# Column attention and feed-forward stage: three column groups in work in a turn instead of two

## The chip, the cores and the metric

The kernel runs on one core of a Trainium2 chip. The metric is the device time of one execution in microseconds (us), the median of several runs. Each engine of the core has its own instruction queue and works through it in order: TensorE (PE; its weight loads are listed as PEld), VectorE (DVE), ScalarE (ACT), GpSimd (POOL) and SyncE (SP). POOL and SP issue the DMA transfers here.

## The reference, cut to what matters

The whole program has two layers on an input of 4 x 64 x 256 x 256 (fp32): a convolutional layer with attention and a gated feed-forward part, and a layer with row attention, column attention and a feed-forward part. The change is in the last stage, which computes this part of the second layer (`h` has batch 4, 256 rows, 256 columns and 64 channels):

```python
def _lin_attn(x, wq, bq, wk, bk, wv, bv, wo, bo):     # 4 heads, one q and one k value a head
    q = elu(x @ wq.T + bq) + 1
    k = elu(x @ wk.T + bk) + 1
    v = x @ wv.T + bv
    q = q / q.mean(axis=3, keepdims=True)             # over the positions of a column
    k = k / k.sum(axis=3, keepdims=True)
    ktv = einsum('brhcd,brhce->brhde', k, v)
    o = einsum('brhcd,brhde->brhce', q, ktv)
    return o @ wo.T + bo

hc = _ln(h.swapaxes(1, 2), cn_g, cn_b)                # columns
h = h + _lin_attn(hc, col_wq, ...).swapaxes(1, 2)
f = _ln(h, fn_g, fn_b)
f = gelu(f @ w1.T + b1) @ w2.T + b2                   # 64 -> 256 -> 64 channels
return moveaxis(h + f, -1, 1)                         # channels first
```

## The kernel before, in words

The program is one function with stages after each other: `stage_a` with the attention and local parts of the first layer, `stage_c1` and `stage_c2` for its feed-forward part, `stage_c3` for the row attention, and `stage_d` for column attention, feed-forward and output. Only `stage_d` differs. `stage_c3` leaves `h` in DRAM as `hd`; `stage_d` reads it.

The stage works on groups of 32 columns: 8 groups in each of 4 batches, 32 groups in all (`seq`: batch `b`, group `g`). A tile `h` holds one group: 128 partitions (rows of one half), 32 columns, two row halves (`rh`) and 64 channels. For each group:

- `load` (L1168): four transfers of 512 KB from SP's queue bring the tile `h`.
- `attn` (L1193): in eight steps the tile is transposed by TensorE (L1203), copied by ScalarE (L1205, `xT`) and multiplied with the query and key weights (L1212, `qk`); beside it `spread` on VectorE takes the mean off 16 x 64 elements at a time and sums the squares (L1178 sum, L1180 centring, L1182 square on ScalarE, L1183 sum of squares). `rstd` (L1186) takes root and reciprocal. Then come the features (`f`, `kz`, L1229 and L1232; the exponential is L696), the product of keys and values (L1238), the sums (L1242), a transpose of q (L1245), the column's small matrix (`zn`, L1259, `mix` with L702, `bdm` L1265), and for each row half the result (a bias product L1271, the product L1274) that is added into `h` in place (L1277). At the end `spread` and `rstd` again give the normalized tiles `xf` (L1288).
- `ffn` (L1291): in eight steps `first` transposes a quarter of `xf` (L1298) and copies it (L1300, `xfT`); four products with `w1` (L1311) go through gelu on ScalarE (L1313, `hg`); `y` takes the transposed `h` (L1319) and the products of `hg` with `w2` (L1322), and VectorE adds the bias and writes it into the output tile `st` (L1324), four columns at a time, with a stride.

`attn` and `ffn` are generators. In turn `n` the main loop (L1342) runs the attention of group `n` and the feed-forward of group `n - 1` in alternation, from one `yield` to the next (`_steps`). A tile framework sets the final order of the instructions on each engine, adds the waits, and gives tiles their buffers: `mm` has six PSUM buffers, `sm` two, `h` three, `xf` five, most others two. In a step of `ffn` the second product takes the gelu values of the same step; the transposes of the next step stand between the two. `st` holds two groups (64 columns); after the second, eight transfers from POOL's queue (L1347) write it out, each of 64 partitions x 32 rows x 64 floats (runs of 256 B).

Of the kernel before, what the change touches and what calls it, by code (L numbers as in the profile page):

```python
# [9 lines left out]
F32 = mybir.dt.float32  # L10
AF = mybir.ActivationFunctionType
ALU = mybir.AluOpType
# [237 lines left out]
def kernel(ctx: ExitStack, tc: tile.TileContext, x, packs, fd, out, off):  # L250
# [8 lines left out]
    def mm():  # L259
        return ps.tile([128, 512], F32, tag="mm", name="mm")  # L260

    def sm():
        return ps.tile([128, 512], F32, tag="sm", name="sm", bufs=2)
# [33 lines left out]
    def bc(ap, n):  # L297

        return ap.unsqueeze(2).to_broadcast([ap.shape[0], ap.shape[1], n])
# [839 lines left out]
    def stage_d():  # L1139
        with ExitStack() as cs:  # L1140
# [25 lines left out]
            V.memset(one, 1.0)  # L1166

            def load(b, g):  # L1168
                h = p.tile([128, 32, 2, C], F32, name="h", bufs=3)
                for rh in (0, 1):  # L1170
                    for j in (0, 1):
                        SY.dma_start(h[:, 16 * j:16 * j + 16, rh, :], hd[b, rh * 128:(rh + 1) * 128, :, 2 * g + j, :])
                return h

            def spread(src, n, s2):

                s1 = p.tile([128, n], F32, tag="ln_s", name="ln_s")
                V.tensor_reduce(s1, src, AX.X, ALU.add)  # L1178
                xc = p.tile([128, n, C], F32, tag="xc", name="xc")
                V.scalar_tensor_tensor(xc, bc(s1, C), -LN_S, src, ALU.mult, ALU.add)  # L1180
                sq = p.tile([128, n, C], F32, tag="ln_sq", name="ln_sq")
                S.activation(sq, xc, AF.Square)  # L1182
                V.tensor_reduce(s2, sq, AX.X, ALU.add)  # L1183
                return xc

            def rstd(s2, n):  # L1186
                s3 = p.tile([128, n], F32, tag="ln_d", name="ln_d")
                S.activation(s3, s2, AF.Sqrt, bias=eps_t, scale=LN_S)
                s4 = p.tile([128, n], F32, tag="ln_r", name="ln_r")
                V.reciprocal(s4, s3)  # L1190
                return s4

            def attn(h, xfs):  # L1193

                qp = p1.tile([128, 32, 32], F32, name="qp")
                v1 = p1.tile([128, 64], F32, name="v1")
                for r in range(8):
                    if r % 2 == 0:
                        k = r // 2
                        spread(h[:, 8 * k:8 * k + 8].rearrange("p c a e -> p (c a) e"), 16, v1[:, 16 * k:16 * k + 16])  # L1200
                    t = mm()
                    for i in range(4):
                        T.transpose(t[:, i * 128:(i + 1) * 128], h[:, r * 4 + i].rearrange("p a e -> p (a e)"), ident)  # L1203
                    xT = p.tile([128, 512], F32, name="xT")
                    S.copy(xT, t)  # L1205
                    yield
                    if r % 4 == 0:
                        qk = sm()


                    for g in range(4):
                        T.matmul(qk[g * 32:(g + 1) * 32, r % 4 * 128:r % 4 * 128 + 128], cwt, xT.rearrange("p (c n) -> p c n", c=4)[:, :, g * 32:(g + 1) * 32],  # L1212
                                 start=True, stop=True)
                    if r % 4 == 3:

                        V.transpose(qp[:, r // 4 * 16:r // 4 * 16 + 16].rearrange("p c m -> p (c m)"), qk)
                rs = rstd(v1, 64)
                u = qp[:, :, 0:16].rearrange("p c (r k) -> p c r k", r=2)
                V.tensor_tensor(u, u, bc4(rs, 2, 8), ALU.mult)
                V.tensor_tensor(u, u, cbq.unsqueeze(1).unsqueeze(1).to_broadcast([128, 32, 2, 8]), ALU.add)  # L1220
                yield
                e = feature(p1, u, [128, 32, 2, 8])
                yield
                f = p1.tile([128, 2, 2, 32, 4], F32, name="f")
# [2 lines left out]
                for rh in (0, 1):  # L1227
                    for k in (0, 1):
                        V.scalar_tensor_tensor(f[:, rh, k], uv[:, rh, :, k * 4:k * 4 + 4], 1.0, ev[:, rh, :, k * 4:k * 4 + 4], ALU.add, ALU.max)  # L1229
                fv = f.rearrange("p r k c h -> p r k (c h)")  # L1230
                kz = p1.tile([128, 2, 128], F32, name="kz")
                V.tensor_tensor(kz.rearrange("p r (c h) -> p r c h", h=4), f[:, :, 1], rs.rearrange("p (c r) -> p r c", r=2).unsqueeze(3).to_broadcast([128, 2, 32, 4]), ALU.mult)  # L1232
                yield

                t = mm()
                for rh in (0, 1):
                    for g in range(4):
                        T.matmul(t[g * 32:(g + 1) * 32, :], kz[:, rh, g * 32:(g + 1) * 32], h[:, 8 * g:8 * g + 8, rh, :], start=(rh == 0), stop=(rh == 1))  # L1238
                qs = sm()
                for k in (0, 1):  # L1240
                    for rh in (0, 1):
# [36 lines left out]
                    yield  # L1278
                for hf in (0, 1):
                    v2 = p.tile([128, 32], F32, name="v2")  # L1280
                    xcs = []
                    for k in (2 * hf, 2 * hf + 1):
                        xcs.append(spread(h[:, 8 * k:8 * k + 8].rearrange("p c a e -> p (c a) e"), 16, v2[:, (k % 2) * 16:(k % 2) * 16 + 16]))
                        yield
                    rs = rstd(v2, 32)
                    for k in (0, 1):
                        xf = p.tile([128, 8, 2, C], F32, name="xf", bufs=5)
                        V.tensor_tensor(xf.rearrange("p c a e -> p (c a) e"), xcs[k], bc(rs[:, k * 16:k * 16 + 16], C), ALU.mult)  # L1288
                        xfs.append(xf)

            def ffn(h, xfs, st, gi):  # L1291


                def first(r):
                    t = mm()
                    xf = xfs[r // 2]
                    for i in range(4):
                        T.transpose(t[:, i * 128:(i + 1) * 128], xf[:, (r % 2) * 4 + i].rearrange("p a e -> p (a e)"), ident)  # L1298
                    xT = p.tile([128, 512], F32, name="xfT")
                    S.copy(xT, t)  # L1300
                    return xT

                yield
                xT = first(0)
                for r in range(8):
                    yield
                    hg = []
                    for i in (0, 1):
                        for rh in (0, 1):
                            t = mm()  # L1310
                            T.matmul(t, w1[rh * 64:(rh + 1) * 64, i * 128:(i + 1) * 128], xT[rh * 64:(rh + 1) * 64], start=True, stop=True)  # L1311
                            g = p.tile([128, 512], F32, tag=f"hg{rh}{i}", name=f"hg{rh}{i}")
                            S.activation(g, t, AF.Gelu, bias=b1[:, i:i + 1])  # L1313
                            hg.append(g)
                    nx = first(r + 1) if r < 7 else None
                    yield
                    y = mm()
                    for i in range(4):
                        T.matmul(y[:, i * 128:(i + 1) * 128], h[:, r * 4 + i].rearrange("p a e -> p (a e)"), ident, is_transpose=True, start=(i == 0), stop=False, skip_group_check=True)  # L1319
                    for i in (0, 1):  # L1320
                        for rh in (0, 1):
                            T.matmul(y[rh * 64:(rh + 1) * 64, :], w2[:, i, :], hg[i * 2 + rh], start=False, stop=(i == 1), skip_group_check=True)  # L1322
                    c = gi * 32 + r * 4
                    V.tensor_scalar(st[:, :, c:c + 4].rearrange("p r c -> p c r"), y.rearrange("p (c r) -> p c r", c=4), K("b2"), None, ALU.add)  # L1324
                    xT = nx

            seq = [(b, g) for b in range(B) for g in range(8)]
            hs = {0: load(*seq[0])}
            xfs = {}
            st = None  # L1330
            for n in range(len(seq) + 1):
                if n + 1 < len(seq):
                    hs[n + 1] = load(*seq[n + 1])
                xfs[n] = []
                ga = attn(hs[n], xfs[n]) if n < len(seq) else None
                gf = None
                if n >= 1:
                    b, g = seq[n - 1]
                    if g % 2 == 0:
                        st = p.tile([128, 128, 64], F32, name="st")  # L1340
                    gf = ffn(hs.pop(n - 1), xfs.pop(n - 1), st, g % 2)
                _steps(ga, gf)  # L1342
                if n >= 1 and g % 2 == 1:
                    for i in range(4):
                        for rh in (0, 1):
                            r = rh * 128 + i * 32
                            G.dma_start(out[b, :, r:r + 32, g // 2 * 64:g // 2 * 64 + 64], st[rh * 64:(rh + 1) * 64, i * 32:(i + 1) * 32])  # L1347

    stage_d()

# [19 lines left out]
```

## Time and profile before

| | |
|---|---|
| time, median of 3 runs | 8939.46 us (8939.42 to 8940.79) |
| profiled execution, its own time | 8937.15 us |
| its span in the profile | 8935.4 us |
| granted TensorE clock, mean | 0.971 |
| begin of the last stage's first load | 6680.0 us |
| last copy into `st` begins | 8907.2 us |
| first of the last eight output issues | 8908.7 us |
| output transfer, issue to landing, median | 13.2 us |

A time in the profile is counted from the start of the span. The page gives busy time by engine for the whole program; a query of stretches gives it for chosen windows; the timeline gives the instructions of an engine in order, with the idle time before each and the engine and line whose end ended it. One group of the last stage takes 68.3 us; the examples are taken from the turn that begins at about 7699 us and the one after it.

### The profile page before, as it was taken

How to read it: one execution, taken by the hardware profiler on the slowest of the kernel's cores; microseconds unless marked ns; L12 is line 12 of the kernel's file. 1: busy time of each engine (PE TensorE's matmuls, PEld its weight loads, DVE VectorE, ACT ScalarE, POOL GpSimd, SP SyncE). 2: the span in 40 equal slices, each digit the busy share in tenths (PEclk: the TensorE clock that was granted, in tenths of full speed). 3: DMA queues.
4: the chain of work that ended last, by engine and by line, in shares of the span. 5: the costliest groups of instructions: out<-in, count | busy, mean ns of one | idle time of the engine just before them, and what ended most of it. 6: DMA issues, size and time to landing. Idle time of an engine off the chain costs nothing. (4 is left out here: it accounts for less than half of the span.)

```text
span 8935.4 us, 143218 instructions
## 1 busy us (share of the span) xinstructions
PE 8237.0 (92%) x57518; PEld 4221.3 (47%) x57518; DVE 5940.4 (66%) x8506; ACT 4587.6 (51%) x7782; POOL 1133.1 (13%) x1828
## 2 busy tenths in 40 slices
PE   8999999699999998999999999999988888989897
PEld 6777777344444443333333344444443333333333
DVE  7766666377777773222222488888877888788776
ACT  4455554455555552222222366666656677667765
POOL 1111111112222221000000011111110000000000
PEclk9999999799999999999999999999998999999998
DMA  7777777799999998888888755555542233233232
GB/s 164 160 187 184 183 185 176 219 357 390 392 390 389 394 378 304 299 296 297 298 298 295 240 170 170 170 170 170 169 121 45 54 70 67 48 76 65 50 67 48
DMA packets 1258502, 1832.48 MB, mean 205 GB/s; under 512 B 335600, under 2 KB 1040112, under 8 KB 1196656
## 3 DMA queue, kind: packets, MB, share of 16 engines
q1 hardware_dynamic: 1053296, 1034.63, 38.5%
q0 software_dynamic: 204544, 788.69, 27.0%
q8 instruction: 456, 7.47, 0.3%
q14 instruction: 206, 1.69, 0.1%
HBM read 967.65 MB, written 788.53 MB: 197 GB/s over the span
## 5 line engine op out<-in xcount | busy, mean ns | idle before, releaser
L915 DVE TENSOR_TENSOR y<-ge,mm 128x512 f32<-128x512 f32 (+1 forms) x640 | 406.0, 634 | 1211.8 <-ACT ge L914 1211.8
L882 PE MATMUL mm<-t,w 128*128 128x512 f32 (+1 forms) x2560 | 1093.7, 566 | 19.1 <-DMA t<-td 19.1
L914 ACT ACTIVATE ge<-mm 128x512 f32<-128x512 f32 (+1 forms) x640 | 354.7, 554 | 1253.8 <-PE mm L889 1253.8
L1313 ACT ACTIVATE hg<-mm,b 128x512 f32<-128x512 f32 x1024 | 631.7, 685 | 331.0 <-PE mm L1311 328.7
L775 PE MATMUL mm<-gp,wc 128*64 128x510 f32 (+1 forms) x3072 | 702.4, 596 | 89.0 <-DVE xm L785 51.0
L620 PEld LDWEIGHTS mm<-wqk,gp 128*128 128x128 f32 x6144 | 728.0, 197 | 99.0 <-issue 60.7
L620 PE MATMUL mm<-wqk,gp 128*128 128x128 f32 x6144 | 761.5, 282 | 1.1 <-POOL gp L589 0.9
L882 PEld LDWEIGHTS mm<-t,w 128*128 128x128 f32 x2560 | 455.2, 189 | 647.5 <-issue 436.9
L1322 PE MATMUL mm<-hg,pack_d 128*64 128x512 f32 x2048 | 579.8, 609 | 101.0 <-ACT hg L1313 101.0
L1311 PE MATMUL mm<-xfT,w 64*128 64x512 f32 x2048 | 637.7, 665 | 2.9 <-ACT xfT L1300 2.2
L830 ACT COPY tb<-mm 128x512 f32<-128x512 f32 x512 | 300.1, 587 | 631.3 <-PE mm L824 631.2
L889 PE MATMUL mm<-t,w 64*64 64x504 f32 (+1 forms) x5120 | 575.6, 555 | 0.0
L824 PE MATMUL mm<-xl,pack_c 64*128 64x512 f32 x2048 | 511.7, 601 | 6.0 <-ACT xl L812 4.6
L775 PEld LDWEIGHTS mm<-gp,wc 128*64 128x64 f32 x3072 | 277.9, 137 | 468.8 <-issue 330.8
L316 ACT ACTIVATE ln_sq<-xn 128x1024 f32<-128x1024 f32 x256 | 274.2, 1071 | 365.9 <-DVE xn L314 365.8
L318 DVE TENSOR_REDUCE ln_v<-ln_sq 128x16 f32<-128x1024 f32 x256 | 312.0, 1219 | 184.2 <-ACT ln_sq L316 184.1
L1324 DVE TENSOR_SCALAR st<-mm,pack_d 128x512 f32<-128x512 f32 x256 | 279.2, 1090 | 171.8 <-PE mm L1322 171.8
L970 PE MATMUL mm<-ya,pack_e 128*64 128x512 f32 x1024 | 381.7, 616 | 11.4 <-DMA ya<-yd 11.4
L1182 ACT ACTIVATE ln_sq<-xc 128x1024 f32<-128x1024 f32 x256 | 266.9, 1055 | 219.8 <-DVE xc L1180 219.7
L828 DVE COPY tb<-mm 128x512 f32<-128x512 f32 x512 | 344.8, 685 | 23.7 <-PE mm L824 18.2
L1311 PEld LDWEIGHTS mm<-xfT,w 64*128 64x128 f32 x2048 | 220.5, 202 | 271.5 <-issue 159.4
L889 PEld LDWEIGHTS mm<-t,w 64*64 64x64 f32 x5120 | 158.1, 132 | 374.4 <-issue 374.4
(458 smaller groups left out, 15178.4 us busy)
## 6 DMA issues: line engine op xcount, KB each, us to landing
t<-td SPq DMA_DIRECT2D x256, 1152.0 KB, 10.0
td<-tb POOLq DMA_DIRECT2D x144, 1024.0 KB, 16.1
td<-tb POOLq DMA_DIRECT2D x288, 512.0 KB, 13.9
yd<-y POOLq DMA_DIRECT2D x128, 1152.0 KB, 10.1
ya<-yd SPq DMA_DIRECT2D x192, 512.0 KB, 5.7
xs<-in_x_dram SPq DMA_DIRECT2D x128, 512.0 KB, 6.8
projd<-pj POOLq DMA_DIRECT2D x256, 256.0 KB, 6.1
gp<-projd SPq DMA_DIRECT2D x128, 512.0 KB, 9.3
```

Of the source, the lines that this page charges most:

```text
L620: T.matmul(qp[:, k * 128:(k + 1) * 128], gp[:, 2 * i + k // 2, at + dx:at + dx + 128], wqk[:, dx, :], start=(dx == 0), stop=(dx == 2))
L775: T.matmul(tv[i * 64:(i + 1) * 64, :, o], wc[2 * pr + i][:, dx, :], gps[i][:, 2 * r:2 * r + 2, i_], start=(dx == 1), stop=False, skip_grou ...
L824: T.matmul(t, inT[q, hf * 128:(hf + 1) * 128], xls[b // 2, s][q, :, 2 * y:2 * y + 2].rearrange("p f y t -> p f (y t)"), start=True, stop=True)
L828: V.tensor_copy(o, i_)
L882: T.matmul(t[:, :n], w[:, 0:128], x_[:, c, :], start=True, stop=False, skip_group_check=True)
L889: T.matmul(t[po:po + 64, :n].rearrange("p (n c) -> p n c", c=64)[:, :, o], w[q:q + 64, 128:192], x_[q:q + 64, c, i_], start=False, stop=Tr ...
L914: S.activation(ge[:, :n], ts[0][k][:, :n], AF.Gelu)
L915: V.tensor_tensor(y[:, c, :].rearrange("p n c -> p (n c)"), ge[:, :n], ts[1][k][:, :n], ALU.mult)
L970: T.matmul(t[b * 64:(b + 1) * 64, :], owT, ya[:, :, 2 * r:2 * r + 2, b * 64:(b + 1) * 64].rearrange("p f y t -> p y f t"), start=True, sto ...
L1311: T.matmul(t, w1[rh * 64:(rh + 1) * 64, i * 128:(i + 1) * 128], xT[rh * 64:(rh + 1) * 64], start=True, stop=True)
L1313: S.activation(g, t, AF.Gelu, bias=b1[:, i:i + 1])
L1322: T.matmul(y[rh * 64:(rh + 1) * 64, :], w2[:, i, :], hg[i * 2 + rh], start=False, stop=(i == 1), skip_group_check=True)
```

## The change

- `attn` is split in `scores` (transposes, `spread`, products, features up to `kz`) and `result` (from the product of keys and values to `xf`). In turn `n` the loop now runs `scores` of group `n + 1`, `result` of group `n` and the feed-forward of group `n - 1`.
- `ffn` is split in `turn` (transposes of `xf` and their copy), `first` (products with `w1`, gelu) and `second` (products with `w2`, copy into `st`). Step `i` counts through all groups; in the place of step `i` stand `turn(i + 2)`, `first(i + 1)` and `second(i)`. In `scores` the transposes of step `r + 1` stand ahead of the break in which the product of step `r + 1` follows.
- `spread` takes two chunks in one call; both sums of squares come after both centrings.
- `st` holds one group (32 columns); four transfers write it, each of 64 partitions x 64 rows x 32 floats (runs of 128 B).
- `h` has four buffers instead of three and is loaded two turns ahead; `xf` has six instead of five.

```diff
-                h = p.tile([128, 32, 2, C], F32, name="h", bufs=3)
+                h = p.tile([128, 32, 2, C], F32, name="h", bufs=4)
...
-            def spread(src, n, s2):
...
+            def spread(h, ks, v):
+                xcs, sqs = [], []
+                for k in ks:
+                    src = h[:, 8 * k:8 * k + 8].rearrange("p c a e -> p (c a) e")
+                    s1 = p.tile([128, 16], F32, tag="ln_s", name="ln_s")
+                    V.tensor_reduce(s1, src, AX.X, ALU.add)
+                    xc = p.tile([128, 16, C], F32, tag="xc", name="xc")
+                    V.scalar_tensor_tensor(xc, bc(s1, C), -LN_S, src, ALU.mult, ALU.add)
+                    sq = p.tile([128, 16, C], F32, tag="ln_sq", name="ln_sq")
+                    S.activation(sq, xc, AF.Square)
+                    xcs.append(xc)
+                    sqs.append(sq)
+                for i, k in enumerate(ks):
+                    V.tensor_reduce(v[:, 16 * i:16 * i + 16], sqs[i], AX.X, ALU.add)
+                return xcs
...
+            def scores(n):
...
+                xT = up(0)
+                spread(h, (0, 1), v1[:, 0:32])
+                yield
+                yield
+                qk = sm()
+                for r in range(7):
+                    if r == 4:
+                        back(0, qk)
+                        qk = sm()
+                    score(r, xT, qk)
+                    xT = up(r + 1)
+                    yield
+                    if r < 5:
+                        if r == 4:
+                            spread(h, (2, 3), v1[:, 32:64])
+                        yield
+                score(7, xT, qk)
+                back(1, qk)
                 rs = rstd(v1, 64)
...
+                fks[n] = f, kz
+
+            def result(n):
+                h = hs[n]
+                f, kz = fks.pop(n)
                 yield
...
+                    xcs = spread(h, (2 * hf, 2 * hf + 1), v2)
+                    yield
                     rs = rstd(v2, 32)
...
-                        xf = p.tile([128, 8, 2, C], F32, name="xf", bufs=5)
+                        xf = p.tile([128, 8, 2, C], F32, name="xf", bufs=6)
...
+            def second(i):
+                n, r = divmod(i, 8)
+                h, hg = hs[n], hgs.pop(i)
+                if r == 0:
+                    sts[n] = p.tile([128, 128, 32], F32, name="st")
...
+                V.tensor_scalar(st[:, :, 4 * r:4 * r + 4].rearrange("p r c -> p c r"), y.rearrange("p (c r) -> p c r", c=4), K("b2"), None, ALU.add)
+                if r == 7:
+                    b, g = seq[n]
+                    for q in (0, 1):
+                        for rh in (0, 1):
+                            y0 = rh * 128 + q * 64
+                            G.dma_start(out[b, :, y0:y0 + 64, g * 32:g * 32 + 32], sts[n][rh * 64:(rh + 1) * 64, q * 64:(q + 1) * 64])
...
+            for n in range(-1, N + 1):
+                if 0 <= n + 2 < N:
+                    hs[n + 2] = load(*seq[n + 2])
+                gs = scores(n + 1) if n + 1 < N else iter(())
+                gr = result(n) if 0 <= n < N else iter(())
+                for r in range(8):
+                    i = 8 * (n - 1) + r
+                    if 0 <= i + 2 < 8 * N:
+                        turn(i + 2)
+                    if 0 <= i + 1 < 8 * N:
+                        first(i + 1)
+                    next(gs, 0)
+                    next(gr, 0)
+                    if 0 <= i < 8 * N:
+                        second(i)
+                    next(gs, 0)
+                    next(gr, 0)
+                _steps(gs, gr)
```

In the changed file the lines named above have new numbers: L1203 becomes L1210, L1205 L1212, L1212 L1219, L1178 L1181, L1180 L1183, L1183 L1189, L1238 L1269, L1242 L1274, L1245 L1277, L1259 L1291, L1271 L1303, L1274 L1306, L1277 L1309, L1298 L1328, L1311 L1339, L1313 L1341, L1319 L1353, L1322 L1356, L1324 L1357, L1347 L1363.

## The prediction

> **What bounds the kernel now.** I read the page's table of engines first, then the stretches of one group each, then the timeline of VectorE and of TensorE inside one such stretch.
>
> ```profile
> span 8935.4 us, 143218 instructions
> PE 8237.0 (92%) x57518; PEld 4221.3 (47%) x57518; DVE 5940.4 (66%) x8506; ACT 4587.6 (51%) x7782; POOL 1133.1 (13%) x1828
> ```
>
> These shares are means over stages. The change is in the last stage only, which starts at 6680 us, so the stretches of that stage decide:
>
> ```profile
> core 0: us, PE busy (x) PEld busy (x) DVE busy (x) ACT busy (x) POOL busy (x), PEclk, DMA share, GB/s
> 7699.40:7767.70 68.30, 61.00 (x349) 26.78 (x349) 54.56 (x68) 47.41 (x69) 6.39 (x7) 0.97 0.44 91
> 7767.70:7836.00 68.30, 61.02 (x351) 26.84 (x351) 54.56 (x68) 47.40 (x69) 2.58 (x4) 0.97 0.15 34
> ```
>
> One column group takes 68.3 us. TensorE looks like the bound with 61.0 us, but part of that is slow clock and waits inside runs of matmuls. At its undisturbed pace (pieces of the chain of waits: L1311 1.92, L1298 0.59, L1212 0.35, L1203 0.59, L1319 0.44, L1322 1.87 us, so 5.76 for each of 8 steps; and 7.8 us for the attention product) it needs 53.9 us. VectorE needs 54.6. So nobody is full: each waits for the other in turn. The timeline of VectorE shows where (start, length, engine, line; in brackets the idle time before, and who ended it):
>
> ```profile
> 7751.30 0.69 DVE L1277 TENSOR_TENSOR h<-mm,h 128x512 f32<-128x512 f32 x1 [2.52 <-PE mm L1274]
> ...
> 7775.29 1.09 DVE L1324 TENSOR_SCALAR st<-mm,pack_d 128x512 f32<-128x512 f32 x1 [1.11 <-PE mm L1322]
> ...
> 7794.57 0.55 DVE L1190 RECIPROCAL ln_r<-ln_d 128x64 f32<-128x64 f32 x1 [1.01 <-ACT ln_d L1188]
> ...
> 7798.85 1.09 DVE L1324 TENSOR_SCALAR st<-mm,pack_d 128x512 f32<-128x512 f32 x1 [1.82 <-PE mm L1322]
> 7800.14 0.90 DVE L1229 SCALAR_TENSOR_TENSOR f<-qp,fe 128x128 f32<-128x128 f32 x4 [0.19 <-ACT fe L696]
> 7801.07 0.42 DVE L1232 TENSOR_TENSOR kz<-f,ln_r 128x256 f32<-128x256 f32 x1
> 7803.62 0.69 DVE L1249 TENSOR_TENSOR zm<-mm,pack_d 128x512 f32<-128x512 f32 x1 [2.13 <-PE mm L1238]
> ```
>
> The reader is to see two parts. From the first addition of the second row half (7751.30) to the end of kz (7801.49) lie 50.2 us in which VectorE is idle only 1.11 + 1.01 + 1.82 + 0.19 = 4.13 us: here it sets the pace. From kz to the next such addition (7819.58) lie 18.1 us in which it mostly waits and TensorE sets the pace. TensorE itself loses 3.3 us once in a turn, waiting for xf, and then runs at half clock:
>
> ```profile
> 7766.32 0.66 PE L1298 MATMUL mm<-pack_k,xf 128*128 128x128 f32 x4 [3.32 <-DVE xf L1288]
> ```
>
> **The change part by part.** I took the order of the changed program's instructions on each engine, with what each waits for.
>
> Instructions: the same arithmetic in the same tiles, and 8 ScalarE table loads per turn as before (1.28 us each). Nothing to add or subtract in busy time, but for the output.
>
> *VectorE's part of a turn.* Its order from the first addition of the second half is: additions, sums and centring of group n, with the copies y(3) to y(7) into st, the score work of group n+1 and the start of that of n+2, and at the end f, y(0), kz. It is the same list of work as in the 50.2 us. What was late must now be early: (a) the second product (L1322, now L1356) takes a gelu of the step before, so no y waits for a gelu of its own step; that takes away the waits of 1.11 and 1.82. (b) xT is transposed a step ahead, and the square root for the 64 rows comes while VectorE does the next group's sums, which takes away the 1.01; the exponential likewise, 0.19. I walked all three engines from t = 0 at that addition with the row durations (1.12 for a sum, 1.13 for a centring, 0.94 between starts for a y copy). TensorE ends y(3) to y(7) and y(0) at 6.8, 12.8, 19.4, 27.2, 34.1 and 42.3; VectorE comes to copy them at 11.5, 18.1, 23.9, 32.7, 39.0 and 44.2. TensorE is ahead by 1.9 to 5.5 us each time, although ScalarE's queue (a square and a table load ahead of the gelus) holds it about 3 us in steps 5 to 7. The bank of a y copied late is next asked for two steps on, so TensorE is not stopped by it until step 0. So all 4.13 us go: 50.2 - 4.1 = 46.1 us.
>
> *TensorE's part.* kz now stands behind y(0) on VectorE, and TensorE waits for it with only L1274 (8 column products, 0.98 us from L1242) left to do. After kz, by the new order: kz product 1.92, L1277 0.28, step 1 with zn 6.0, L702 0.43, step 2 up to y 3.45, first half 1.95, y 2.31, second half 1.95. Against the old 18.1 us: 0.98 less for the column products, two more score products and transposes (2 x 0.94), 0.56 less because L1311 no longer waits inside (2.48 against 1.92): +0.34, so 18.4. Sum 64.5; I allow 0.2 for hand-offs: 64.7 us a turn instead of 68.3.
>
> *Output.* st of one group is written in runs of 32 floats, 128 B, where it was 64, 256 B. The trace has no 128 B row. POOL's issue goes by rows: 0.55 us for 1024 (L1125), 1.10 for 2048 (L1347), so about 2.2 for 4096; four in a turn, 8.8 us of an engine that else has one memset. For the transfer the nearest row is the end of the kernel: the last eight issues, 16384 rows of 256 B, kept the 16 DMA engines busy for about 21.5 us, 21 ns a row. [...] By the row a turn has 21.5 us of output[...], and the loads of h about 8 us more[...]. It is hidden beside the turn's work, and st's buffer is asked for only a turn later. It counts at the end alone: 27.1 us from the last y to the end before[...]; I take 27.1, the nearest row.
>
> The strided copy into st has 1090 ns, and an addition of the same size without stride (L1277) 684. Half the stride could cost anything from 684 to some 1500 (as much again above); I take 1090, the same operation's row.
>
> *The loads of h* come two turns ahead with four buffers; the load is asked for when the buffer's old group is done, and has some 50 us for about 8. POOL's memset for zn stands ahead of the previous output. Neither is on the path.
>
> *Clock.* Slices of 2 us (the column before the last two is the granted clock) show what follows on the idle 3.32 us:
>
> ```profile
> 7763.40:7765.40 2.00, 0.00 (x0) 0.00 (x0) 1.97 (x4) 0.74 (x2) 0.00 (x0) 1.00 1.01 232
> 7765.40:7767.40 2.00, 1.08 (x8) 0.94 (x8) 2.00 (x3) 0.33 (x1) 0.00 (x0) 0.91 0.20 45
> 7767.40:7769.40 2.00, 1.95 (x6) 0.84 (x6) 2.00 (x2) 1.89 (x3) 0.00 (x0) 0.50 0.00 0
> ```
>
> Half clock, for some 3.5 us by the same slices a turn earlier (0.50, then 0.81): 1.75 us of work lost. In the new order the longest time without a streaming product is before the kz product, 42.3 to 45.7, with 0.98 us of column products in it. By the nearest row (3.32 us idle, half clock in each turn) it would fall, for 1.75 us a turn[...]. I take none and keep 1.75 for the range.
>
> *The sum*, on the profiled span. The first "addition of the second half" lies at 6726.7 before. The changed order does six VectorE operations of group 1 earlier (6.8 us, 2.3 of it in idle time): 6731.2. The first turn lacks five y copies: 60.0, to 6791.2. 30 turns of 64.7: 8732.2. Then y(3) to y(7) of the last-but-one step and eight steps without attention, 4.81 us each as in the old last turn: 67.4 us from my walk, and 27.1: 8826.7. The profiled execution took 1.75 us more than its span, and the median of the three runs is 2.3 above it: 8831 us, 1.2% less. About 0.2%, 18 us, is what a measurement of this kernel can tell from no change.
>
> **The rivals.** *Half clock before the kz product in every turn*: 30 x 1.75 on top, 8883. For it: the old turn shows it after the same length. [...]
>
> *A cheaper st copy at the smaller stride*: six copies lie in VectorE's part, 6 x 0.4 x 30 = 72 less, 8759. Nothing in the profile speaks for it but the gap between 1090 and 684.
>
> *A new wait instead of the old*: VectorE waits for ScalarE. ScalarE is busy 47.4 of now 64.7 us in one queue; where the four pairs of L1189 each wait 1 us for a square behind a table load and two gelus (2.9 and 1.2 us), the 4.1 us are back: 68.3 a turn, 8939. My walk leaves 0.1 to 4 us there, so a little of it may come, all of it hardly. The same number results if TensorE's early transposes buy nothing because VectorE was the bound all along: that is the case that the change doesn't do what it says.
>
> *Slower: output in 128 B rows.* 1024 rows per DMA engine and turn, and 8 us of loads. From (68.3 - 8)/1024 = 59 ns a row, the output sets the turn and the kernel is slower. At three times the old row, 64 ns, a turn is 73.5 us, and the time 8831 + 30 x 8.8 = 9095. Against: it would have to triple while the bytes halve.
>
> **How the numbers follow.** Forecast 0.57; half clock 0.15; cheaper copy 0.11; a new wait 0.09, of which 0.05 within 0.2%, 0.02 faster and 0.02 slower; slow output 0.08. Faster: 0.57 + 0.15 + 0.11 + 0.02 = 0.85; same 0.05; slower 0.10. The range goes from the cheaper copy, 8755, to a little over the half clock, 8900; it leaves out the last two cases.
>
> **What would show it.** Right: stretches of one group of 64 to 65 us, VectorE with no idle over 0.3 us from the second half's additions to kz, L1356 with no wait for L1341, no TensorE wait for xf, L1357 at 1.09 us, output issues of 2.2 us. Wrong: VectorE waiting for ln_sq or ln_d (the new wait), PEclk of 0.5 after kz, L1357 under 1 us, a first y copy of a group waiting for the output (slow rows).

## The result, and the profile after

The changed kernel takes 8823.01 us (median of 4 runs, 8820.8 to 8826.35), the kernel before 8939.44 us (4 runs): a ratio of 0.9871, interval 0.9854 to 0.9888. The prediction was 8831 us, in a range of 8755 to 8900. The profiled execution took 8823.91 us. First its page and the stretch of one turn:

```profile
span 8822.1 us, 143300 instructions
PE 8201.0 (93%) x57518; PEld 4222.1 (48%) x57518; DVE 5913.9 (67%) x8506; ACT 4597.9 (52%) x7781; POOL 1205.3 (14%) x1828
```

```profile
core 0: us, PE busy (x) PEld busy (x) DVE busy (x) ACT busy (x) POOL busy (x), PEclk, DMA share, GB/s
7705.13:7769.98 64.85, 59.80 (x350) 26.74 (x351) 53.70 (x67) 47.66 (x69) 6.63 (x5) 0.97 0.33 66
```

A turn went from 68.30 to 64.85 us with the same instructions in it. TensorE's busy time still contains a stretch of half clock. The timeline of VectorE in this turn (start, length, engine, line; in brackets the idle time before and who ended it):

```profile
7705.13 0.69 DVE L1309 TENSOR_TENSOR h<-mm,h 128x512 f32<-128x512 f32 x1 [0.81 <-PE mm L1306]
...
7716.69 1.09 DVE L1357 TENSOR_SCALAR st<-mm,pack_d 128x512 f32<-128x512 f32 x1
...
7741.38 0.51 DVE L1196 RECIPROCAL ln_r<-ln_d 128x64 f32<-128x64 f32 x1
...
7747.89 0.90 DVE L1256 SCALAR_TENSOR_TENSOR f<-qp,fe 128x128 f32<-128x128 f32 x4
...
7749.64 0.40 DVE L1258 TENSOR_TENSOR kz<-f,ln_r 128x256 f32<-128x256 f32 x1
...
7753.53 0.69 DVE L1281 TENSOR_TENSOR zm<-mm,pack_d 128x512 f32<-128x512 f32 x1 [3.08 <-PE mm L1269]
...
7769.98 0.69 DVE L1309 TENSOR_TENSOR h<-mm,h 128x512 f32<-128x512 f32 x1 [0.81 <-PE mm L1306]
```

The copy, the reciprocal and the features, which in the old turn had 1.11, 1.01, 1.82 and 0.19 us of idle time ahead of them, have no bracket any more. VectorE's part of the turn, from the first addition of the second row half to the end of kz, went from 50.2 to 44.9 us (7705.13 to 7750.04). The rest, to the next such addition, went from 18.1 to 19.9 us. The timeline of TensorE and the 2 us slices (the column before the last two is the granted clock) show why it grew:

```profile
7748.23 1.23 PE L1274 MATMUL sm<-pack_k,f 128*128 128x1 f32 x8 [1.10 <-DVE f L1256]
7750.19 3.28 PE L1269 MATMUL mm<-h,kz 128*32 128x512 f32 x16 [0.72 <-DVE qr L704]
```

```profile
7748.00:7750.00 2.00, 1.21 (x8) 1.04 (x8) 2.00 (x7) 1.99 (x3) 1.87 (x2) 0.89 0.96 150
7750.00:7752.00 2.00, 1.81 (x12) 0.58 (x16) 0.41 (x4) 0.33 (x1) 0.00 (x0) 0.50 0.96 164
7752.00:7754.00 2.00, 2.00 (x18) 0.70 (x10) 0.47 (x1) 0.13 (x1) 1.64 (x1) 0.76 0.98 168
```

The product with kz takes 3.28 us where it took 1.92 in the kernel before:

```profile
7733.35 1.92 PE L1238 MATMUL mm<-h,kz 128*32 128x512 f32 x16 [0.32 <-DVE kz L1232]
```

The clock has fallen to half. If it went from whole to half and back once, the means 0.89, 0.50 and 0.76 put the fall at about 7749.6 and the return at about 7753.0, some 3.4 us later. Slices of half a microsecond (0.56 from 7749.5, 0.53 from 7752.5) give 7749.56 and 7752.97, so 3.41 us. Last, the output tile:

```profile
L1363 POOL DMA_DIRECT2D out_dram<-st x128: 1635/1635/1672, 6835.4 to 8811.5; - x128
...
DMA to landing us min/median/max: 7.0/9.0/11.3
```

Each issue of 4096 rows costs POOL 1.64 us, and no copy into st waits for the output inside a turn.

### The profile page after: what moved, and what is told of

Same layout as the page of the kernel before. It is cut to its first block, busy times and chain, and to the rows that moved or that the text cites. A ratio compares the mean times of both kernels' runs of the same rounds, so it can differ in the third digit from the quotient of the medians.

```text
span 8822.1 us, 143300 instructions
## 1 busy us (share of the span) xinstructions
PE 8201.0 (93%) x57518; PEld 4222.1 (48%) x57518; DVE 5913.9 (67%) x8506; ACT 4597.9 (52%) x7781; POOL 1205.3 (14%) x1828
## 5 line engine op out<-in xcount | busy, mean ns | idle before, releaser
L1341 ACT ACTIVATE hg<-mm,b 128x512 f32<-128x512 f32 x1024 | 645.2, 689 | 47.3 <-PE mm L1339 45.6
L1339 PE MATMUL mm<-xfT,w 64*128 64x512 f32 x2048 | 623.7, 626 | 25.7 <-DVE h L1309 22.6
L1356 PE MATMUL mm<-hg,pack_d 128*64 128x512 f32 x2048 | 496.8, 606 | 0.0
L1363 POOL DMA_DIRECT2D out_dram<-st x128 | 209.1, 1638 | 1725.0 <-DVE st L1357 1640.9
L1339 PEld LDWEIGHTS mm<-xfT,w 64*128 64x128 f32 x2048 | 225.6, 185 | 255.2 <-issue 112.1
L1357 DVE TENSOR_SCALAR st<-mm,pack_d 128x512 f32<-128x512 f32 x256 | 277.7, 1085 | 101.3 <-PE mm L1356 101.3
```

The costliest lines, as they stand in the source:

```text
L1339: T.matmul(t, w1[rh * 64:(rh + 1) * 64, k * 128:(k + 1) * 128], xT[rh * 64:(rh + 1) * 64], start=True, stop=True)
L1341: S.activation(g, t, AF.Gelu, bias=b1[:, k:k + 1])
L1356: T.matmul(y[rh * 64:(rh + 1) * 64, :], w2[:, k, :], hg[k * 2 + rh], start=False, stop=(k == 1), skip_group_check=True)
L1357: V.tensor_scalar(st[:, :, 4 * r:4 * r + 4].rearrange("p r c -> p c r"), y.rearrange("p (c r) -> p c r", c=4), K("b2"), None, ALU.add)
```

## The experiments

The questions were which part of the change the gain comes from (e1, e2, e3), whether VectorE sets the pace (e4), why the clock falls (e5, e6, e9, e10), what would be next (e7, e8, e11), and whether the turn's length is set by the clock itself (e12). The times of the kernel before beside them were 8936.58 us (e1 to e4), 8935.77 (e5 to e8), 8939.66 (e9 to e11) and 8938.81 (e12).

**e1: three groups, without the look-ahead.** The products with w1, the gelu and the products with w2 of a step are in the same step again, the transposes one step ahead, as before the change.

```diff
-                    if 0 <= i + 2 < 8 * N:
-                        turn(i + 2)
-                    if 0 <= i + 1 < 8 * N:
-                        first(i + 1)
+                    if 0 <= i < 8 * N:
+                        if i == 0:
+                            turn(0)
+                        first(i)
+                    if 0 <= i and i + 1 < 8 * N:
+                        turn(i + 1)
```

> Three groups in a turn as in the changed kernel, but the feed-forward step is the old one: second(i) takes the gelus of first(i) of the same step, turn(i + 1) stands between. Theory (the pace is set by VectorE's part from the second half's additions to kz, and the look-ahead is what takes the waits for y out of it): the waits for y of 1.1 and 1.8 us come back, some 2.9 us a turn, 64.9 to 67.8, about 8910 us. Rival (three groups alone fill VectorE's queue with other work, so the y copies are late anyway): within 20 us of 8823.

Measured: 8842.18 us (8841.65 to 8845.46), ratio 0.9893 (0.9878 to 0.9908). The theory that the look-ahead removes VectorE's waits fell: 19 us are lost without it, of 116. VectorE's and TensorE's timelines of a turn:

```profile
7708.85 0.69 DVE L1309 TENSOR_TENSOR h<-mm,h 128x512 f32<-128x512 f32 x1 [0.79 <-PE mm L1306]
...
7729.06 1.22 DVE L1189 TENSOR_REDUCE v<-ln_sq 128x16 f32<-128x1024 f32 x1 [0.24 <-ACT ln_sq L1185]
...
7747.39 1.10 DVE L1357 TENSOR_SCALAR st<-mm,pack_d 128x512 f32<-128x512 f32 x1
...
7752.73 0.42 DVE L1258 TENSOR_TENSOR kz<-f,ln_r 128x256 f32<-128x256 f32 x1
...
7774.01 0.69 DVE L1309 TENSOR_TENSOR h<-mm,h 128x512 f32<-128x512 f32 x1 [0.79 <-PE mm L1306]
```

```profile
7744.74 1.65 PE L1356 MATMUL mm<-hg,pack_d 128*64 128x512 f32 x4 [1.70 <-ACT hg L1341]
...
7753.31 1.04 PE L1269 MATMUL mm<-h,kz 128*32 128x512 f32 x2
7754.28 1.07 PE L1356 MATMUL mm<-hg,pack_d 128*64 128x512 f32 x2
7755.29 1.92 PE L1269 MATMUL mm<-h,kz 128*32 128x512 f32 x14
```

TensorE waits 1.70 us for a gelu of its own step, as it did in the kernel before; but VectorE's copy of that product has no wait, because VectorE comes to it later. VectorE's part is 44.3 us here with 0.24 us of idle time: its waits are gone without the look-ahead. (e1 keeps the paired sums of squares and the added buffers; no run takes these apart from the third group.) The turn is 65.16 us, only 0.3 more than with the look-ahead, but here the product with kz runs at full clock. At the same clock the look-ahead is worth more: e5 below has turns of 63.5 us with the clock whole, about 1.7 us less than e1. The 18.0 us between the two spans lie half in the turns (kz of the last group ends 8.6 us later) and half behind them (9.4 us, in the last group's feed-forward, which has nothing beside it to fill the wait for a gelu).

**e2: the look-ahead alone, with two groups in work.** The transposes two steps ahead and the first products one step ahead, within the eight steps of one group.

```diff
                 yield
-                xT = first(0)
+                xTs = {0: turn(0), 1: turn(1)}
+                hgs = {0: first(xTs[0])}
                 for r in range(8):
                     yield
+                    if r + 2 < 8:
+                        xTs[r + 2] = turn(r + 2)
+                    if r + 1 < 8:
+                        hgs[r + 1] = first(xTs[r + 1])
```

> Two groups in a turn as before, attention unchanged, output tile of two groups; only the feed-forward looks ahead inside a group: turn(r + 2), first(r + 1), second(r). Theory: the waits for y (2.9 us a turn) go, those for ln_d (1.0) and for xf at the turn's begin (3.3 us of TensorE and the half clock after it) stay: 68.3 to about 65.4, 8939 to some 8850. Rival (the look-ahead needs three groups, because at each turn's begin it starts empty and nothing covers the first products): within 20 us of 8939.

Measured: 9131.5 us (9128.68 to 9136.27), ratio 1.0217 (1.0201 to 1.0232). Both expectations were wrong; it is 195 us slower than before. Its turns take 72.7 to 75.4 us. TensorE's timeline in one of 72.7, and a slice:

```profile
7712.71 1.94 PE L1298 MATMUL mm<-pack_k,xf 128*128 128x128 f32 x8 [7.77 <-DVE xf L1288]
7714.58 3.79 PE L1308 MATMUL mm<-xfT,w 64*128 64x512 f32 x8
```

```profile
7710.00:7712.00 2.00, 0.00 (x0) 0.00 (x0) 1.97 (x3) 0.27 (x1) 0.00 (x0) 0.50 0.00 0
```

The wait for xf at the change of groups, 3.3 us in the kernel before, is 7.8 us: at the end of a group the steps ahead are used up, only products with w2 are left, and the next group's xf isn't there. Then the clock is at half. A look-ahead needs work ahead. In the changed kernel, where the third group gives such work and the steps count on from group to group, TensorE waits nowhere for xf.

**e3: the kernel before with the output tile of one group.** Runs of 128 B, four transfers after each group; nothing else.

```diff
-                    if g % 2 == 0:
-                        st = p.tile([128, 128, 64], F32, name="st")
-                    gf = ffn(hs.pop(n - 1), xfs.pop(n - 1), st, g % 2)
+                    st = p.tile([128, 128, 32], F32, name="st")
+                    gf = ffn(hs.pop(n - 1), xfs.pop(n - 1), st, 0)
```

> The kernel before with only the output tile of one group: four transfers of 64 x 64 x 32 floats after each group instead of eight of 64 x 32 x 64 after two. Theory: the turns keep 68.3 us and only the end shrinks, 27.1 to 18.4 us as seen in the changed kernel: 8939 to about 8930. Rival (short runs or the smaller stride matter in the turn): over 15 us away from 8930.

Measured: 8929.34 us (8922.61 to 8937.21), ratio 0.9991 (0.9985 to 0.9998). As expected: nothing in the turns, some us at the end. In its profile the time from the last copy's end to the end of the span is 18.7 us, where it was 27.1.

**e4: the changed kernel with a copy into st that isn't strided.** It puts the values into other places of the output; the copy and the transfers are of the same size.

```diff
-V.tensor_scalar(st[:, :, 4 * r:4 * r + 4].rearrange("p r c -> p c r"), ...)
+V.tensor_scalar(st[:, 16 * r:16 * r + 16].rearrange("p r c -> p (r c)"), y, ...)
```

> The changed kernel, but the copy of y into st is written without a stride, so the output's elements stand in other places. Theory (VectorE sets the pace; six of the eight copies lie in its part): the copy falls from 1.09 to about 0.69 us, 0.4 x 6 x 31 = 74 us less, about 8750. Rival (TensorE sets the pace there too): under 20 us less.

Measured: 8774.08 us (8768.27 to 8777.37), ratio 0.9817 (0.9801 to 0.9834): 49 us less than the changed kernel, not 74. VectorE does set the pace. Of its timeline the copy and a new wait:

```profile
7754.75 0.74 DVE L1357 TENSOR_SCALAR st<-mm,pack_d 128x512 f32<-128x512 f32 x1
...
7785.15 0.90 DVE L1256 SCALAR_TENSOR_TENSOR f<-qp,fe 128x128 f32<-128x128 f32 x4 [0.51 <-ACT fe L696]
```

The turns now differ: 62.44 us, 2.4 less than 64.85 as expected, where the product with kz runs at full clock (1.92 us), and 64.06, where it doesn't (2.5 to 3.4 us). They mostly take turns. So the clock took back most of what was missing: 1.6 us in about every second turn.

**e5: the sums over 128 columns.** The same sums as before, in 128 equal columns, so that TensorE streams more in the stretch ahead of the product with kz.

```diff
-T.matmul(qs[:, k:k + 1], fv[:, rh, k], K0("ones"), ...)
+T.matmul(qs[:, k * 128:k * 128 + 128], fv[:, rh, k], one, ...)
...
-V.reciprocal(rz, qs[:, 1:2])
+V.reciprocal(rz, qs[:, 128:129])
```

> The kernel after, with the sums of the scores' features (L1274) written over 128 columns each instead of one. Question: why TensorE's clock falls to half before the kz product. Theory 1 (TensorE streams too little in the 3 us before it: waits and one-column products): with 128-column sums it streams more there, L1269 goes back from 3.28 us to about 1.92, a turn from 64.9 to 63.5 us, the whole to about 8783 us (30 turns by 1.36 us). Theory 2 (what counts is the waits between the products, not their width): the clock falls as before, time within 5 us of 8823; the sums' own extra length, about 0.2 us after the last f, is hidden by kz.

Measured: 8794.64 us (8791.55 to 8796.96), ratio 0.9841 (0.9827 to 0.9856), 28 us less than the changed kernel. TensorE's timeline in two turns in a row:

```profile
7598.99 1.34 PE L1274 MATMUL sm<-one,f 128*128 128x128 f32 x8 [1.08 <-DVE f L1256]
7600.95 3.62 PE L1269 MATMUL mm<-h,kz 128*32 128x512 f32 x16 [0.63 <-DVE qr L704]
...
7664.21 1.34 PE L1274 MATMUL sm<-one,f 128*128 128x128 f32 x8 [1.08 <-DVE f L1256]
7666.18 1.92 PE L1269 MATMUL mm<-h,kz 128*32 128x512 f32 x16 [0.63 <-DVE qr L704]
```

The two turns have the same instructions and the same waits, to 0.01 us. In the first the slices of 2 us show a clock of 0.75 and 0.50 from 7600 to 7604; from 7725 to 7733, around the product of the turn after the second, they show 1.00. Behind the two products at the start of the stage and ahead of the last one there are 29 with this gap. 10 of them ran partly at half clock, and their turns take 65.1 to 65.2 us; the turns of the other 19 take 63.5, one of them 63.8. These 29 turns gained 23.6 of the 30.8 us between the two spans; the rest was gained ahead of them. So narrow sums are one cause of the fall.

What sets the two kinds of turn apart is in e5's trace: the time of each change of clock. All changes measured in its turns lie on one grid, whole multiples of 3.413 us apart, to 0.001 us. The changed kernel's trace shows the same step: 29 stretches at half clock in its turns, each 3.413 us long, their starts 64.853 us apart (6841.61 to 8657.50). In the 10 turns with a fall, TensorE's gap (from the end of the products with w2 to the product with kz) began 0.06 to 0.43 us behind a point of this grid; in the 19 without, 0.65 us or more. As 63.5 us are not a whole multiple of 3.413, the gap lies elsewhere on the grid in each turn.

**e6: kz ahead of the features of k = 0.** Both features of k = 1 and kz stand first, so that kz isn't behind the copy of y(0).

```diff
-for rh in (0, 1):
-    for k in (0, 1):
-        V.scalar_tensor_tensor(f[:, rh, k], ...)
-V.tensor_tensor(kz..., f[:, :, 1], ...)
+for k in (1, 0):
+    for rh in (0, 1):
+        V.scalar_tensor_tensor(f[:, rh, k], ...)
+    if k == 1:
+        V.tensor_tensor(kz..., f[:, :, 1], ...)
```

> The kernel after, with both f of k = 1 and then kz ahead of the two f of k = 0, so that kz stands ahead of the last y copy on VectorE. Theory 1 (the turn is VectorE's run up to kz, then TensorE's chain): kz ends 1.09 us (the copy) and about 1.4 us (two f) earlier less what the product zm (L1281) must wait for, and the two f then lie in VectorE's idle end of the turn; 1.1 to 2.5 us a turn, 30 turns, so 8750 to 8790 us. If the shorter gap on TensorE also keeps the clock whole, 1.36 us a turn more: down to 8710. Theory 2 (the sums, which need the two f of k = 0, come into the chain instead): within 10 us of 8823.

Measured: 8770.36 us (8766.33 to 8771.64), ratio 0.9814 (0.9799 to 0.9828). Its turn is 63.04 us; TensorE's timeline:

```profile
7721.32 0.38 PE L1275 MATMUL sm<-pack_k,f 128*128 128x1 f32 x2 [1.48 <-DVE f L1257]
7721.75 1.92 PE L1270 MATMUL mm<-h,kz 128*32 128x512 f32 x16
```

From the end of the last products with w2 (7719.84) to the product with kz it is 1.9 us, not 3.05 as in the changed kernel (7747.14 to 7750.19), and the clock stays whole in every steady turn. Of the 1.81 us gained a turn, 1.36 are the clock. Theory 1 holds in the time, but most of it came through the clock, on which I had counted only for the lower end.

**e7 and e8: the next group's centrings behind this group's sums.** In e7 the centrings of the score's layernorm take their factor from a tile worked out from the sums (it holds the same -1/64), so that they lie behind kz; e8 has kz first as well.

```diff
+ng = p.tile([128, 1], F32, name="ng")
+V.tensor_scalar(ng, qs[:, 0:1], 0.0, -LN_S, ALU.mult, ALU.add)
+gates[n] = ng
...
-V.scalar_tensor_tensor(xc, bc(s1, C), -LN_S, src, ALU.mult, ALU.add)
+V.scalar_tensor_tensor(xc, bc(s1, C), m, src, ALU.mult, ALU.add)
...
-spread(h, (0, 1), v1[:, 0:32])
+if r == 0:
+    spread(h, (0, 1), v1[:, 0:32], gates.get(n - 1, -LN_S))
+if r == 1:
+    spread(h, (2, 3), v1[:, 32:64], gates.get(n - 1, -LN_S))
```

> The kernel after, with the score's layernorm centrings of the next group made to wait for the sums of this group's scores (their factor is read from a tile worked out from the sums), so that they lie in the stretch in which VectorE waits for TensorE's product chain. Theory 1 (VectorE is idle for some 11 us of a turn behind kz, and its run up to kz sets the turn): about 10 us of VectorE's work leave the run; part delays the mix's own steps on VectorE; turn 56 to 61 us, 30 turns, so 8560 to 8710 us. Theory 2 (the moved work only comes in the way of zm, st and h in the product chain, so that the chain grows by what the run loses, or TensorE's 54 us bind at once): turn 62 to 66 us, 8740 to 8860 us.

> The two foregoing edits together: centrings of the next group behind this group's sums, and kz ahead of the f of k = 0. Theory 1: the gains add, 1 to 2.5 us a turn under the centrings alone. Theory 2: once the centrings are moved TensorE's own work sets the turn, and kz's place is worth under 10 us.

Measured: e7 8745.04 us, ratio 0.9784 (0.9768 to 0.9801); e8 8747.37 us, ratio 0.9789 (0.9774 to 0.9803). In e7 VectorE's part falls from 44.9 to 36.5 us (7672.58 to 7709.06), and the rest grows from 19.9 to 24.8. VectorE waits inside its part now, and again behind kz:

```profile
7704.24 0.72 DVE L1224 STREAM_TRANSPOSE qp<-sm 128x512 f32<-128x512 f32 x1 [3.25 <-PE sm L1219]
...
7712.07 1.10 DVE L1361 TENSOR_SCALAR st<-mm,pack_d 128x512 f32<-128x512 f32 x1 [3.01 <-PE mm L1360]
```

It waits for TensorE's own queue, which in this turn is busy 57.1 of 61.29 us. So most of the moved 8.4 us came back, theory 2's way; the time lies at its lower end. kz's place is worth nothing there, as e8's theory 2 had it. The clock is whole in the turn shown, but not in all: e7 and e8 mostly have three or four turns of 61.3 us, then one of 64.0 and one of 62.7, in which it falls. In e7 the slices show 0.50 from 7228.5 to 7235 us, in a turn of 64.0.

**e9 and e10: wide sums where the clock is whole already.** e9 is e1 with e5's edit, e10 is e6 with it.

> Three groups without the look-ahead in the feed-forward step, and with the sums (L1274) over 128 columns. There the kz product already ran at full clock with narrow sums. Theory 1 (wide sums help only by the clock they keep up): no change against the three groups alone, 8842 within 6 us. Theory 2 (wide sums help by something else, order or shorter waits): about 28 us less, as on the kernel after, so about 8814.

> The kernel after with both: kz ahead of the f of k = 0, and sums over 128 columns. Theory 1 (kz first already keeps the clock whole, so there is nothing left for the width): 8770 within 6 us. Theory 2 (the two gains are of different kinds and add): about 8742.

Measured: e10 8768.67 us (8767.07 to 8772.87), ratio 0.9808 (0.9792 to 0.9825), against 8770.36 for e6: no gain, theory 1. e9 8857.42 us (8854.31 to 8858.44), ratio 0.9907 (0.9893 to 0.9922), 15 us more than e1. There six of the eight wide sums moved behind the product with kz, and the turn grew from 65.16 to 65.80 us. Neither theory had this. The order changed with the width there, so e9 is no clean test; e10 is one, and it shows that the width gains nothing where the clock doesn't fall.

**e11: half of e7, with kz first.** Only the centrings of the second half (2, 3) wait for the sums; their call moves from r == 4 to r == 1, as in e7.

> The kernel after with kz first, and with only the second half of the score's centrings of the next group made to wait for this group's sums. Theory 1 (with all centrings moved TensorE's own queue sets the turn, and moved work stood in the way of bdm and the second additions; half of it is a better share): turn 60 to 61.2 us, so 8710 to 8742 us. Theory 2 (VectorE's run again sets the turn): turn about 62 us, 8750 to 8765 us.

Measured: 8723.45 us (8716.11 to 8725.37), ratio 0.9757 (0.9742 to 0.9771): the shortest of all kernels here, 100 us less than the changed kernel. Every steady turn is 61.2 us, a hair above the 60 to 61.2 of theory 1, split into 40.0 and 21.2. But the reason that theory 1 gave, the better share, is not what gains over e7 and e8: their turns with the clock whole take 61.3 us too. What they lose are the turns of 62.7 and 64.0 us, some 27 us in all in e7 and 22 in e8, and e11's clock falls in none of its steady turns.

**e12: more work for VectorE.** Half of the copy of y(3) is written a second time. Theory 1 is that a turn keeps to 19.0 steps of the grid shown in e5 (19 x 3.413 = 64.85 us).

```diff
 V.tensor_scalar(st[:, :, 4 * r:4 * r + 4].rearrange("p r c -> p c r"), ...)
+if r == 3:
+    V.tensor_scalar(st[:, :, 12:14].rearrange("p r c -> p c r"), y[:, 0:256]..., ...)
```

> The kernel after with more work for VectorE: half of the copy of y(3) into st is written a second time, some 0.5 us in the part of the turn in which VectorE sets the pace; the order on all engines else stays. Theory 1 ([...] in the kernel after every turn settles at 64.85 us[...] with the kz product partly at half clock; without the half clock it would be 63.5): the turn stays at 64.85 us, the half clock takes less of the kz product (L1269 about 2.8 us instead of 3.28), and the time stays within 5 us of 8823 although 30 times 0.5 us of work came in. Theory 2 (the half clock costs a fixed 1.36 us each turn and the turn is simply VectorE's run and TensorE's chain): the turn becomes about 65.35 us, the time about 8838 us, L1269 stays at 3.28.

Measured: 8825.82 us (8824.68 to 8829.07), ratio 0.9876 (0.9859 to 0.9892), 2.8 us more than the changed kernel, and not 15. The second copy takes 0.67 us, a little more than expected; a fixed cost of the clock would have made 20 us of it. Two turns are 129.70 us, twice 64.85 again. The products with kz in the changed kernel, then in e12:

```profile
7555.65 3.27 PE L1269 MATMUL mm<-h,kz 128*32 128x512 f32 x16 [0.73 <-DVE qr L704]
7620.50 3.27 PE L1269 MATMUL mm<-h,kz 128*32 128x512 f32 x16 [0.73 <-DVE qr L704]
7685.34 3.27 PE L1269 MATMUL mm<-h,kz 128*32 128x512 f32 x16 [0.72 <-DVE qr L704]
```

```profile
7556.97 1.93 PE L1269 MATMUL mm<-h,kz 128*32 128x512 f32 x16 [0.73 <-DVE qr L704]
7621.16 3.24 PE L1269 MATMUL mm<-h,kz 128*32 128x512 f32 x16 [0.73 <-DVE qr L704]
7686.66 1.92 PE L1269 MATMUL mm<-h,kz 128*32 128x512 f32 x16 [0.73 <-DVE qr L704]
```

In the changed kernel all are alike and 64.85 us apart. In e12 the clock falls in every second turn, and the starts are 64.19 and 65.50 us apart. I had expected the same shorter half clock in every turn; it is a whole one in every second. The falls are 129.71 us apart, 38.0 steps of the same grid. The time agrees with a turn locked to the grid, theory 1, not with a fixed cost in every turn.

## Why the prediction was right, point by point

The mechanism held in the main: with three groups in work VectorE's waits went, and the turn went from 68.3 to 64.85 us. Of the reasons given for it one was wrong, the step on the clock failed, and the sum came out closer than its terms.

- **VectorE's part, 46.1 us forecast: 44.9.** All four waits went, as said, but the reason given for two of them, step (a), the gelu of the step before, is not the cause: e1 has no look-ahead and no such waits. What removes them is the new order of e1, which puts the third group's score work between VectorE's copies. The 1.2 us beyond the forecast come partly from instructions that depend on each other and now have others between them: behind a step of qp the next instruction starts 0.73 us later where it needs that step's result (L1219 and L1220 of the kernel before), and 0.59 where it doesn't (L1247 and L1248 of the changed one). The rest is not accounted for.
- **TensorE's part, 18.4 us forecast: 19.9.** This step failed, and it is the one on the clock. I had the row that said 1.75 us a turn and set it aside; no trace or run here had shown a ground for that. The rival of half clock happened in every steady turn, with 1.36 us instead of 1.75, because the fall comes 0.63 us ahead of the product with kz. The gap before this product is 3.05 us, 1.23 of it products of one column, and the clock fell about 2.4 us after the last product of 512 columns. The 3.413 us ahead of the fall (7746.15 to 7749.56) held 1.0 us of the products with w2 and all of the one-column products. So this window (a stretch of 3.413 us between two points of the grid shown in e5) was not empty. From the third group's product on, the changed kernel, e4 and e12 have 60 falls in their turns. All came behind a window with at most 1.24 us of TensorE's time outside the one-column sums; behind windows at whole clock with 1.34 us or more the clock stayed. The figures hold for these runs alone: one fall of e7 (at 7228.48) came behind a window in which TensorE was busy 3.2 us, 1.5 of it with bias products (L1307) of one row of weights.
- **The turn, 64.7 us forecast: 64.85.** The agreement is partly luck. The errors of the two parts nearly cancel; and e5's turns with the clock whole show 63.5 us for nearly the same work. The grid shows in the turn's length: in the traces the changes of clock in this stage lie on a grid of 3.413 us in every run, in e8 and e11 all but one. 64.85 us are 19.0 windows. The changed kernel did not start at this length. Its first turns took 65.1 to 65.2 us, and the product with kz shortened from turn to turn:

```profile
7036.15 3.60 PE L1269 MATMUL mm<-h,kz 128*32 128x512 f32 x16 [0.73 <-DVE qr L704]
7101.35 3.43 PE L1269 MATMUL mm<-h,kz 128*32 128x512 f32 x16 [0.74 <-DVE qr L704]
7166.40 3.33 PE L1269 MATMUL mm<-h,kz 128*32 128x512 f32 x16 [0.75 <-DVE qr L704]
7231.35 3.28 PE L1269 MATMUL mm<-h,kz 128*32 128x512 f32 x16 [0.73 <-DVE qr L704]
```

A turn longer than 19 windows brings the gap later against the grid (it began 0.35, 0.69, 0.88 and 0.99 us behind a point of it in these four), so the fall lies earlier ahead of the product, less of the half clock meets it, and the turn shortens until it is 19 windows. That is the lock: 29 falls, 64.853 us apart. A little added work can then be free, as the 0.67 us of e12; no run shows how much. The falls of the old kernel are 20.0 windows apart from turn to turn (68.27 us), but its turn of 68.28 us kept drifting against the grid and grew to 69.1 near the end, so it was not settled in the same way. The turns of e1, e6 and e11, whose product with kz is at full clock, are 19.1, 18.5 and 17.9 windows.

- **The ends.** First turn 60.0 us forecast, 63.8 measured (there too the clock falls to half, 0.70 in the mean); the end part 67.4 against 67.6. The tail behind the last copy, forecast 27.1 us by the row of 256 B, was 18.4: the output kept the DMA engines busy for some 12 us (a share of 0.87 from 8806 to 8820), 12 ns for each row of 128 B, where it was 21 ns for 256 B (0.81 from 8908 to 8934 in the kernel before). The row of 256 B, taken unchanged, put the transfer some 9 us too high, and the tail came 8.7 us shorter. e3 shows nearly the same tail on the old kernel, 18.7. POOL's issue took 1.64 us, not 2.2; it is hidden.
- **Sum**, in span: +0.6 us at the first addition, +3.8 in the first turn, -0.5 over the turns, +0.2 in the end part, -8.7 in the tail: 8822.1 instead of 8826.7. The -0.5 is luck too: 29 of the 30 turns average 64.91 us, 6 us too much in all, and the last, which has no scores beside it, took 58.2, 6.5 less than the sum gave it.
- **The rivals.** Half clock: happened. Cheaper copy: did not (1.09 us); e4 shows that it would have counted, with 49 us. New wait of VectorE for ScalarE: none inside the turn. Slow rows: the reverse.

## What to carry to other kernels

When two engines wait for each other in turn, more independent work in each one's queue can remove the waits; here deeper look-ahead within one item did not, and lost more at the item's ends than it gained inside (195 us). Where the granted clock falls once in each turn, look for the gap first: moving one small operation (kz, e6) ended the falls, streaming wider (e5) ended two in three (19 of 29), and until they end small gains and losses elsewhere may not show in the time at all (e12). With VectorE's run shortened further, look at the clock again: moving half of the work (e11) beat moving all of it (e7, e8) by 22 to 24 us, though their turns at whole clock are equally long.

## What the runs showed of the hardware that I had not expected

- In the traces of the 14 runs the clock changed on a grid of 3.413 us, all but two of the changes in the turns. So the same instructions with the same waits, to 0.01 us, met half clock in one turn and full clock in the next (e5: L1269 at 3.62 and 1.92 us), by where the grid fell on the gap (a point of it 0.06 to 0.43 us ahead of the gap, or 0.65 and more).
- The clock fell with 1.23 us of one-column products in the 3.05 us before; 128 columns in their place, at the same length of the gap, kept it up in 19 of 29 turns.
- Turns settled at one length after some eight turns, 64.85 us to within 0.05 us, 19.0 steps of that grid, and took a copy of 0.67 us more without growing on average.
- A copy of 128 x 512 from PSUM into st took 1.09 us at a stride of 128 B as at 256 B, and 0.74 without stride.
- At the end of the two kernels 16384 rows of 128 B kept the 16 DMA engines busy for some 12 us, as many of 256 B for some 21: 12 and 21 ns a row on each engine. Between these two sizes the transfer went nearly with the bytes.
